# A four-layer graph network on one core: x3 transposed through HBM, softmax and RMS factors spread from compact bf16 parts

## The chip, the core and the metric

The kernel runs on one core of a Trainium2 chip. A core has a matrix engine (TensorE, PE in the profile), which multiplies a stationary operand held in its array (loaded by a weight load, PEld) with a moving operand, and writes to PSUM; VectorE (DVE); ScalarE (ACT); GpSimd (POOL); and SyncE (SP), which here issues every DMA. Each engine works through its own queue in order. The metric is the device time of one execution in microseconds, the median of several.

## What is computed

There are 32 graphs of 512 nodes with 256 features. `adj` holds zeros and ones, with ones on the diagonal. Every graph goes through four layers, and each ends in `x = layernorm(x + layer(x))`. All of it is float32.

```
L0: q,k,v = x@Wq+bq, x@Wk+bk, x@Wv+bv        # 8 heads of 32
    p = softmax(where(adj>0, q@k.T/sqrt(32), -9e15));  L0 = (p@v)@Wo + bo
L1: L1 = relu(((1+eps)*x + adj@x)@W1 + b1)@W2 + b2              # hidden 512
L2: h = (eps*x + adj@x)@W1 + b1                                 # hidden 1024
    L2 = silu(h * rsqrt(mean(h*h) + 1e-6) * rms_weight)@W2 + b2
L3: xn = layernorm(x)*gamma + beta;  A = s_out * adj * s_in
    L3 = softplus(xn@W_self + ((I - A)@xn)@W_neigh)
```

x3 is the input of layer 3. The two factors of this text are the reciprocal of the softmax sum, one per head and node, and the `rsqrt` of the mean square in L2 (the RMS factor), one per node.

## The kernel before

The 512 nodes are four tiles of 128 (`NT`), the 256 features two chunks of 128 (`DC`). The function `graph(b)` does not issue anything. It records operations, each with an engine (or two to choose from), a cost in nanoseconds, what it reads and writes, its buffers and a stage name. The class `Order` (L60) then puts the operations of all 32 graphs in one order with a list scheduler: among those that can start within 100 ns of the earliest on an engine, the one with the lowest key goes first. A key is the graph's number times `PERIOD`, plus a place between the earliest and the latest time at which the operation could stand within its graph (`LATE`), plus a number per stage (`LEAD`); `TURN` is the cost that the scheduler puts down when TensorE goes from whole-array products to row tiles (scores) or column tiles (p@v), `TURN_DUE` a penalty on such a turn, `HASTE` moves the last graph. So stages of several graphs lie interleaved on every engine, and the order that results is the program's order.

The parts that matter here, with their lines:

- **Scores and softmax** (`attend`, L751): for each half of the heads (`g`) and each node tile four products of 32 rows run side by side in the array (L766, tile `sc`). VectorE adds the mask and takes the row extremum (L790), ScalarE takes the exponential and its sum `rs` (L804). VectorE turns 32x32 blocks of the result (L840), SP writes them to an HBM scratch `via` (L852) and reads them back as `pT` (L864), and TensorE multiplies with v in 32-column tiles (L883, tile `po_att`).
- **Softmax factor** (stage `rinv`, L897 to L957), once for each `g`: VectorE takes the reciprocal of 16 sums per row (L903) and splits it into three bf16 parts whose sum keeps the float32 precision (L912, L919). The parts are written with gaps into a 128 x 4 x 128 tile `parts`, which TensorE transposes in four products (L930, `pm_t`); the result is copied (L937 or L938); one product with the 0/1 selector `sel_r` spreads it over the 32 rows of each head (L943, `pr_r`, 512 columns); it is copied to `oT` (L533), and VectorE multiplies `po_att` into it (L955). `oT` is what the product with Wo reads (L970, `po<-wo,oT`).
- **RMS factor** (stage `rms`, L1245 to L1298): TensorE sums squares (L1251, `pm`), VectorE and GpSimd make the factor `rr`, VectorE writes four diagonal matrices (L1275, `diag`), and one float32 product of a matrix of ones with them (L1281, `pb`) puts the factor of each node into every row. VectorE multiplies it into eight blocks of `gT` (L1289), ScalarE takes silu in two halves (L1304), then comes W2 (L970, `po<-w,gT`).
- **x3 transposed** (stage `x3T`, L1332 to L1360): eight float32 transposes on TensorE (L1341, `pt`), two copies out of PSUM by VectorE or ScalarE (L1352, L1356) into `xnT`, which the first product of layer 3 reads (L1369, `pz`). It is followed by the product with adj (L1411, `pa_l`).
- **Transposes by DMA that exist already**: for every graph but the first, `load_blocks` (L577) reads x and adj from HBM in 32x32 blocks whose runs are 128 bytes, four DMAs a matrix, and VectorE turns the blocks in place (L665 for x, L614 for adj).

```
def load_blocks(dst, src, q):
    v = src.rearrange("(i r) (m a c) -> a r m i c", r=32, a=4, c=32)
    nc.sync.dma_start(dst[32 * q : 32 * q + 32].rearrange("r m (i c) -> r m i c", c=32), v[q])
```

Of the kernel before, what the change touches and what calls it, by code (L numbers as in the profile page):

```python
# [9 lines left out]
F32 = mybir.dt.float32  # L10
BF16 = mybir.dt.bfloat16
AF = mybir.ActivationFunctionType
ALU = mybir.AluOpType
# [3 lines left out]
P = 128  # L17
# [2 lines left out]
RMS_EPS = 1e-6  # L20
HEADS = 8

PERIOD = 55957
LEAD = {
    "adjT": 178900, "agg1": 2600, "agg2": -164100, "degree": 73600, "diag": -115600,
    "lap": -139200, "ln0": -34000, "ln1": -303400, "ln2": 108900, "ln3": 310600, "load": 67000,
    "move": -461200, "pv": -4100, "pz": -65900, "qk": 9400, "rinv": -98900, "rms": -72400,
    "scores": -4600, "silu": 110900, "softplus": 52400, "v": 134300, "w11": 4200, "w12": -5600,
    "w21": -3500, "w22": -9100, "wo": -16600, "x3T": -71100, "xT": -89500,
}  # L30


# [27 lines left out]
class Order:  # L60
# [8 lines left out]
    WAIT = 70  # L69
    TABLE, TABLE_DUE = 1300, 9000  # L70

    TURN = {"whole": 93, "row": 200, "col": 93}
    TURN_DUE = 6000
    LATE = 0.85
    HASTE = 12445

    def __init__(self):
        self.ops = []
# [204 lines left out]
def kernel(  # L283
# [53 lines left out]

    ident_b = const.tile([P, P], BF16, name="ident_b")  # L340
    nc.vector.tensor_copy(ident_b, ident)
    parts = []
    for i in range(2):
        t = const.tile([P, NT, P], BF16, name=f"parts{i}")
        nc.gpsimd.memset(t, 0.0)
        parts.append(t)
    id_js = ident.rearrange("p (j s) -> p j s", s=HD)
    block = const.tile([P, HPG], F32, name="block")
    nc.vector.tensor_reduce(block, id_js, axis=AX.X, op=ALU.add)
    rows_js = const.tile([P, HPG], F32, name="rows_js")  # L350
    nc.vector.tensor_reduce(rows_js, id_js[:, :, 0:3], axis=AX.X, op=ALU.add)
    rows_of = const.tile([P, 1], F32, name="rows_of")
    nc.vector.tensor_reduce(rows_of, rows_js, axis=AX.X, op=ALU.add)
    sel_r = const.tile([P, HPG, HD], BF16, name="sel_r")
    nc.vector.tensor_scalar_mul(
        sel_r, block.unsqueeze(2).to_broadcast([P, HPG, HD]), rows_of[:, 0:1]
    )

    order = Order()

# [138 lines left out]
    def graph(b):  # L499
        first, last = b == 0, b == B - 1  # L500
        early = b < 1
        def op(ways, r=(), w=(), hold=()):
            order.op(b, ways, r, w, hold, stage[0])
# [3 lines left out]
        def bank(name):  # L507
            return Buf(ps, [P, 512], F32, "m", f"{name}_{b}", 4)

        def tmp(shape, tag, bufs, name=None, dtype=F32):  # L510
            return Buf(sb, shape, dtype, tag, f"{name or tag}_{b}", bufs)

        def pe(cost, fn, r, w, *hold, turn="whole"):

            op([("PE", cost, fn, {"turn": turn})], r, w, hold)

        def dve(cost, fn, r, w, port=False):
            op([("DVE", cost, fn, {"port": 1} if port else {})], r, w)
# [7 lines left out]
        def either(r, w, dve_way, act_way, port=False):  # L526
            op([("DVE", dve_way[0], dve_way[1], {"port": 1} if port else {}), ("ACT", act_way[0], act_way[1], {})], r, w)
# [32 lines left out]
        def small(name, bufs=2, shape=None):  # L560
            return Buf(sb, shape or [P, NT], F32, "s_" + name, f"{name}_{b}", bufs)
# [186 lines left out]

        oT = tmp([P, DC, N], "oT", 1)

        def attend(g):  # L751


            mx = small("mx", 2, [P, NT, HPG])
            rs = small("rsum", 2, [P, NT, HPG])
            po = bank("po_att")
            pTs = []
            for t in range(NT):
# [21 lines left out]
                for j in range(HPG):  # L780
# [5 lines left out]
                    else:  # L786
# [18 lines left out]
                            row(), row(), AF.Exp,  # L805
                            bias=mx[:, t, j : j + 1],
                            scale=-1.0,
                            accum_out=rs[:, t, j : j + 1],
                        ),
                        [(mx, t, j)], [(pq, j), (rs, t, j)],  # L810
                        table="exp",
                    )
                stage[0] = "move"
# [81 lines left out]
                )  # L895

            stage[0] = "rinv"  # L897

            tj = [(t, j) for t in range(NT) for j in range(HPG)]
            rv = small("rv", 2, [P, NT, HPG])  # L900
            dve(
                240,
                lambda: nc.vector.reciprocal(rv(), rs()),  # L903
                [(rs, t, j) for t, j in tj], [(rv,)],
            )
            part = parts[g].rearrange("p t (j s) -> p t j s", s=HD)
            left = rv
            for r in range(3):
                dst = part[:, :, :, r]
                dve(  # L910
                    190,
                    lambda dst=dst, left=left: nc.vector.tensor_copy(dst, left()),  # L912
                    [(left,)], [("parts", g), ("parts", g, r)], port=True,
                )
                if r < 2:
                    rest = small("rest", 2, [P, NT, HPG])
                    dve(
                        180,
                        lambda dst=dst, left=left, rest=rest: nc.vector.tensor_tensor(  # L919
                            rest(), left(), dst, ALU.subtract  # L920
                        ),
                        [(left,), ("parts", g, r)], [(rest,)], port=True,
                    )
                    left = rest
            pm_t = Buf(ps, [P, N], BF16, "m", f"pm_t_{b}", 4)
            mT = tmp([P, N], "mT", 2, dtype=BF16)

            def tr():
                for t in range(NT):
                    nc.tensor.transpose(  # L930
                        pm_t[:, t * P : (t + 1) * P], parts[g][:, t, :], ident_b
                    )

            pe(240, tr, [("parts", g)] + [("parts", g, r) for r in range(3)], [(pm_t,)], mT)
            either(
                [(pm_t,)], [(mT,)],
                (420, lambda: nc.vector.tensor_copy(mT(), pm_t())),  # L937
                (590, lambda: nc.scalar.copy(mT(), pm_t())),  # L938
            )
            pr_r = bank("pr_r")  # L940
            pe(
                130,
                lambda: nc.tensor.matmul(  # L943
                    pr_r(),
                    lhsT=sel_r.rearrange("p j e -> p (j e)"),
                    rhs=mT(),
                    start=True,
                    stop=True,
                ),
                [(mT,)], [(pr_r,)], oT,  # L950
            )
            evacuate(lambda: oT[:, g, :], pr_r, [(pr_r,)], [(oT, g)])
            dve(
                700,
                lambda: nc.vector.tensor_tensor(oT[:, g, :], po(), oT[:, g, :], ALU.mult),  # L955
                [(po,)], [(oT, g)],
            )  # L957

        def pair_sum(lhs, lhs_k, w, w_k, nk, y, step):

# [101 lines left out]
        values()  # L1062
        attend(0)
        attend(1)
        stage[0] = "wo"
        pair_sum(oT, lambda k: (oT, k), wo, "wo", DC, y, DC)

# [200 lines left out]
        rr = small("rr")  # L1268
        rsqrt(rr, ms, [(ms,)], [(rr,)])

        diag = tmp([P, NT, P], "sq", 2, "diag")

        def spread():
            for t in range(NT):
                nc.vector.tensor_scalar_mul(diag[:, t, :], ident, rr[:, t : t + 1])  # L1275

        dve(880, spread, [(rr,)], [(diag,)])
        pb = bank("pb")
        pe(
            870,  # L1280
            lambda: nc.tensor.matmul(  # L1281
                pb(), lhsT=ones, rhs=diag().rearrange("p t q -> p (t q)"), start=True, stop=True
            ),
            [(diag,)], [(pb,)],
        )
        for m in range(C2):
            dve(
                750,
# [41 lines left out]
        r3 = small("r3")  # L1330
        rsqrt(r3, v3e, [(v3e,)], [(r3,)])
        stage[0] = "x3T"  # L1332
        xnT = tmp([P, DC, N], "hT", 1, "xnT")
        for c in range(DC):
            pt = bank("pt")
            for rt in row_tiles:
                part = slice(rt[0] * P, (rt[-1] + 1) * P)

                def tr_x3(c=c, rt=rt, pt=pt):
                    for t in rt:  # L1340
                        nc.tensor.transpose(  # L1341
                            pt[:, t * P : (t + 1) * P], x3[:, t, c * P : (c + 1) * P], ident
                        )

                pe(115 * len(rt), tr_x3, [(x3, t) for t in rt], [(pt, rt[0])], xnT)
                src = lambda part=part, pt=pt: pt[:, part]
                dst = lambda part=part, c=c: xnT[:, c, part]
                op(
                    [
                        (  # L1350
                            "DVE", 160 + 133 * len(rt),
                            lambda src=src, dst=dst: nc.vector.tensor_copy(dst(), src()), {},  # L1352
                        ),
                        (
                            "ACT", 190 + 100 * len(rt),
                            lambda src=src, dst=dst: nc.scalar.copy(dst(), src()), {},  # L1356
                        ),
                    ],
                    [(pt, rt[0])], [(xnT, c, t) for t in rt],
                )  # L1360

        stage[0] = "pz"
        zy = tmp([P, NT, 2 * D], "aT", 1, "zy")
# [160 lines left out]
```

## Time and profile before

| what | value |
|---|---|
| median of three runs | 3435.14 us (3434.87 to 3435.78) |
| the profiled execution's own time | 3424.53 us |
| its span, first to last instruction | 3422.5 us |
| PE / DVE / ACT / POOL busy | 98% / 78% / 59% / 25% of the span |
| mean busy share of the 16 DMA engines by the one queue that carries the data | 66.9% |
| HBM read, written | 364.27 MB, 276.82 MB |

A row of a group of instructions reads: line, engine, operation, tiles written and read, shape, count, then busy time, mean duration of one, and the idle time of the engine just before them with what ended it. A matmul's own duration holds its way through the array, and the next one starts before it ends; so the time that one costs is read from the starts of two neighbours in the timeline, whose rows give start, duration, line, tiles and count. Each float32 product of the program stands in the profile as two passes.

### The profile page before, as it was taken

The page shows a single profiled execution, that of the slowest core. Times are in us where ns is not written, and L with a number is a line of the kernel's source. Part 1 is how long each engine was busy: PE and PEld are TensorE (multiplying, and loading weights), DVE is VectorE, ACT ScalarE, POOL GpSimd, SP SyncE. Part 2 cuts the span into 40 slices and gives each one's busy share as a digit, 9 for nine tenths or more (in the row PEclk, how much of TensorE's full clock was granted, in tenths as well). Part 3 has the DMA queues.
Part 4 walks back from the last instruction along what each step waited for, and adds up shares of the span by engine and source line. Part 5 has one row for each costly group of instructions (what it writes and reads, how often), then busy time and mean ns, then how long its engine had stood idle before and what let it go on. Part 6 is the DMA issues. An engine that isn't in the chain of part 4 may idle for free.

```text
span 3422.5 us, 55733 instructions
## 1 busy us (share of the span) xinstructions
PE 3368.0 (98%) x20000; PEld 2030.2 (59%) x20000; DVE 2664.6 (78%) x6241; ACT 2033.0 (59%) x4124; POOL 857.9 (25%) x615
## 2 busy tenths in 40 slices
PE   8999999999999999999999999999999999999997
PEld 5556655665655666556655655565566655565565
DVE  7788878778777788777787777887877877778755
ACT  6555666556666556666566655666565666556633
POOL 1222222222232222222132321222222223212231
PEclk9999999999999999999999999999999999999999
DMA  5777766667767667666677666676766767766710
GB/s 152 231 220 215 207 195 191 197 186 213 198 186 199 194 197 202 195 189 197 187 212 198 186 191 200 194 204 190 197 191 191 215 191 196 192 196 180 207 40 13
DMA packets 622868, 644.74 MB, mean 188 GB/s; under 512 B 410752, under 2 KB 446976, under 8 KB 590848
## 3 DMA queue, kind: packets, MB, share of 16 engines
q1 hardware_dynamic: 622592, 641.19, 66.9%
q8 instruction: 157, 2.57, 0.3%
q14 instruction: 119, 0.97, 0.1%
HBM read 364.27 MB, written 276.82 MB: 187 GB/s over the span
## 4 chain that ended last, share of the span: by engine, by line
PE 89%; DMA 5%; DVE 3%; issue 1%; SPq 1%; ACT 1%; POOL 0%; DVEq 0%; POOLq 0%
PE po L970 22%; PE ph L1148 13%; PE pg L1165 7%; PE sc L766 7%; PE pq L694 7%; PE pa L1165 7%; PE pz L1369 7%; PE pa_l L1411 6%; PE po_att L883 6%; DMA adjT<-in_adj_dram 4%; PE pv L735 3%; PE pb L1281 1%; PE pt L1341 1%; DVE pq L790 1%; PE pm L1251 1%
## 5 line engine op out<-in xcount | busy, mean ns | idle before, releaser
L804 ACT ACTIVATE pq<-pq,mx 128x512 f32<-128x512 f32 x1024 | 728.1, 712 | 255.9 <-DVE mx L790 161.0
L790 DVE CUSTOM_DVE_ANT_0 pq<-sc,bias 128x512 f32<-128x512 f32 x1024 | 664.0, 684 | 151.0 <-PE sc L766 95.3
L840 DVE STREAM_TRANSPOSE pq<-pq 128x2048 f32<-128x2048 f32 x248 | 572.2, 2307 | 82.7 <-ACT pq L804 82.5
L970 PE MATMUL po<-w,gT 128*128 128x256 f32 x2048 | 466.6, 381 | 0.5 <-ACT gT L1304 0.5
L1165 PE MATMUL pg<-hT,w 128*128 128x512 f32 x1024 | 465.9, 598 | 0.0
L970 PEld LDWEIGHTS po<-w,gT 128*128 128x128 f32 x2048 | 384.4, 190 | 88.8 <-issue 36.9
L540 POOL TENSOR_TENSOR ssq<-ssq,sq 128x512 f32<-128x512 f32 x220 | 281.1, 1278 | 292.1 <-ACT sq L1241 285.1
L1023 POOL TENSOR_TENSOR rstd<-ve,nhalf 128x4 f32<-128x4 f32 x132 | 143.7, 1089 | 767.9 <-DVE ve L1018 767.8
L1165 PEld LDWEIGHTS pg<-hT,w 128*128 128x128 f32 x1024 | 189.4, 190 | 218.6 <-issue 206.0
L766 PE MATMUL sc<-kT,qT 32*128 32x512 f32 x2048 | 292.1, 640 | 5.3 <-DVE nmr L1030 4.4
L883 PEld LDWEIGHTS po_att<-pT,v 128*32 128x32 f32 x8192 | 215.8, 110 | 94.9 <-issue 66.8
L883 PE MATMUL po_att<-pT,v 128*32 128x128 f32 x8192 | 250.2, 274 | 0.0
L1369 PE MATMUL pz<-wsn,xnT 128*128 128x512 f32 x512 | 236.7, 597 | 0.4 <-DVE xnT L1352 0.4
L540 POOL TENSOR_TENSOR sp<-sp,y 128x1024 f32<-128x1024 f32 x31 | 73.0, 2355 | 645.6 <-PE pg L1165 572.5
L1165 PE MATMUL pa<-hT,w 128*128 128x512 f32 x512 | 233.3, 599 | 0.3 <-DVE hT L532 0.3
L1148 PE MATMUL ph<-adjT,y_att 128*128 128x512 f32 x512 | 227.3, 596 | 1.4 <-DVE adjT L1130 1.4
L1148 PE MATMUL ph<-adjT,y 128*128 128x512 f32 x512 | 228.5, 598 | 0.0
L970 PE MATMUL po<-w,aT 128*128 128x256 f32 x1024 | 227.6, 379 | 0.0
L1411 PE MATMUL pa_l<-zy,adjT 128*128 128x256 f32 x1024 | 226.6, 379 | 0.0
L1411 PEld LDWEIGHTS pa_l<-zy,adjT 128*128 128x128 f32 x1024 | 194.5, 190 | 40.8 <-issue 15.5
L970 PEld LDWEIGHTS po<-w,aT 128*128 128x128 f32 x1024 | 192.0, 190 | 26.5 <-ACT pq L804 0.8
L804 ACT ACTIVATION_READ_ACCUMULATOR pq<-pq,mx 128x1 f32 x1024 | 191.9, 187 | 0.0
(150 smaller groups left out, 4991.6 us busy)
## 6 DMA issues: line engine op xcount, KB each, us to landing
via<-pq SPq DMA_DIRECT2D x992, 256.0 KB, 4.3
pT<-via SPq DMA_DIRECT2D x248, 1024.0 KB, 5.7
adj<-in_adj_dram SPq DMA_DIRECT2D x32, 1024.0 KB, 5.1
adjT<-in_adj_dram SPq DMA_DIRECT2D x124, 256.0 KB, 4.7
x<-in_x_dram SPq DMA_DIRECT2D x32, 512.0 KB, 3.9
xT<-in_x_dram SPq DMA_DIRECT2D x124, 128.0 KB, 4.1
out_dram<-sp SPq DMA_DIRECT2D x31, 512.0 KB, 5.2
w<-in_L_gnn_W_dram SPq DMA_DIRECT2D x2, 1024.0 KB, 6.5
```

The costliest lines, as they stand in the source:

```text
L540: lambda: nc.gpsimd.tensor_tensor(dst(), dst(), src(), ALU.add), {},
L694: nc.tensor.matmul(pq(), lhsT=w[:, c, m * P : (m + 1) * P], rhs=xT[:, c, :], start=(c == 0), stop=(c == DC - 1),)
L766: nc.tensor.matmul(sc[:, j, :], lhsT=qT[hp, g, t * P : (t + 1) * P], rhs=kT[hp, g, :], start=True, stop=True,)
L790: lambda t=t, j=j, sc=sc, row=row: nc.vector.tensor_tensor_reduce(out=row(), in0=sc[:, j, :].rearrange("p (a n) -> p a n", a=4), in1=bias[ ...
L804: lambda t=t, j=j, row=row: nc.scalar.activation(row(), row(), AF.Exp, bias=mx[:, t, j : j + 1], scale=-1.0, accum_out=rs[:, t, j : j + 1],),
L840: lambda pq=pq: nc.vector.transpose(pq().rearrange("p a j c s -> p (a j c s)"), pq().rearrange("p a j c s -> p (a j c s)"),),
L883: nc.tensor.matmul(po[j * HD : (j + 1) * HD, t * P : (t + 1) * P], lhsT=v[:, c, h * HD : (h + 1) * HD], rhs=pT[:, :, j, c, :], start=(c == 0),
L970: nc.tensor.matmul(po[:, i * D : (i + 1) * D], lhsT=lhs[:, k, t * P : (t + 1) * P], rhs=w[:, k, :], start=(i == 0 and k == 0), stop=(i == ...
L1148: nc.tensor.matmul(ph(), lhsT=xin[:, m, c * P : (c + 1) * P], rhs=adjT[:, m, :], start=(m == 0), stop=(m == NT - 1),)
L1165: nc.tensor.matmul(pa(), lhsT=w[:, c, m * P : (m + 1) * P], rhs=hT[:, c, :], start=(c == 0), stop=(c == DC - 1),)
L1369: nc.tensor.matmul(pz(), lhsT=xnT[:, c, t * P : (t + 1) * P], rhs=wsn[:, c, :], start=(c == 0), stop=(c == DC - 1),)
L1411: nc.tensor.matmul(pa[:, i * D : (i + 1) * D], lhsT=adjT[:, m, t * P : (t + 1) * P], rhs=zy[:, m, D : 2 * D], start=(m == 0), stop=(m == N ...
```

## The change

Three things are changed, and the scheduler's numbers with them.

1. x3, for every graph but the last, is written by one DMA to an HBM scratch tensor `x3d` and read back by four `load_blocks` DMAs; VectorE turns the blocks in place. Its tile `xnT` takes the buffer of `xT` instead of that of `hT`.
2. The softmax factor is made once per graph for both halves (32 sums per row). Its three bf16 parts lie side by side in 96 columns; one transpose gives 96 rows, and eight products of 128 columns, four per half, spread them with a wider selector. `po_att` itself is now copied to `oT` at once, and the product with the factor is taken from PSUM later.
3. The RMS factor goes the same way: three parts in 12 columns, one transpose, four products of 128 columns with a selector `sel_t`. The diagonal matrices and the float32 product of ones are gone.

`PERIOD`, all of `LEAD`, `TURN`, `TURN_DUE`, `LATE` and `HASTE` have other values, so the order of all engines is another one.

```diff
-PERIOD = 55957
+PERIOD = 65676
...
-    TURN = {"whole": 93, "row": 200, "col": 93}
-    TURN_DUE = 6000
-    LATE = 0.85
-    HASTE = 12445
+    TURN = {"whole": 93, "row": 290, "col": 150}
+    TURN_DUE = 500
+    LATE = 0.06
+    HASTE = -1245
...
+    NX = 2 * NT * HPG
+    sel_r = selector(NX, HD, "sel_r")
+    sel_t = selector(NT, P, "sel_t")
...
             stage[0] = "rinv"
+            evacuate(lambda: oT[:, g, :], po, [(po,)], [(oT, g)])
+
+        def split(src, n, name):
+            parts = tmp([P, 3, n], "p_" + name, 2, name + "p", dtype=BF16)
...
+            pe(
+                65,
+                lambda: nc.tensor.transpose(
+                    pm_t[0 : 3 * n, :], parts().rearrange("p r x -> p (r x)"), ident_b
+                ),
...
+            mT = split(rv, NX, "sums")
+            for g in range(2):
...
+                    for t in range(NT):
+                        x = (g * NT + t) * HPG
+                        nc.tensor.matmul(
+                            pr_r[:, t * P : (t + 1) * P],
+                            lhsT=sel_r[0 : 3 * NX, x : x + HPG].rearrange("p j e -> p (j e)"),
+                            rhs=mT[0 : 3 * NX],
+                            start=True,
+                            stop=True,
+                        )
...
-        dve(880, spread, [(rr,)], [(diag,)])
...
+        mT = split(rr, NT, "rms")
+            for t in range(NT):
+                nc.tensor.matmul(
+                    pb[:, t * P : (t + 1) * P],
+                    lhsT=sel_t[0 : 3 * NT, t],
+                    rhs=mT[0 : 3 * NT],
+                    start=True,
+                    stop=True,
+                )
...
+            x3d = Buf(dr, [N, D], F32, "x3d", f"x3d_{b}", 2)
+                    lambda: nc.sync.dma_start(
+                        x3d().rearrange("(t p) d -> p t d", p=P), x3()
+                    ),
...
+                        "SP", 4900, lambda q=q: load_blocks(xnT(), x3d(), q),
...
+                lambda: nc.vector.transpose(
+                    xnT().rearrange("p c i -> p (c i)"), xnT().rearrange("p c i -> p (c i)")
+                ),
```

## The prediction

> **What bounds the kernel now.** I read the page's busy shares first, then the three steady windows of about one graph each, then TensorE's timeline.
>
> ```profile
> PE 3368.0 (98%) x20000; PEld 2030.2 (59%) x20000; DVE 2664.6 (78%) x6241; ACT 2033.0 (59%) x4124; POOL 857.9 (25%) x615
> ...
> 1500.00:1607.00 107.00, 106.01 (x631) 63.44 (x624) 83.80 (x196) 65.33 (x131) 27.01 (x19) 1.00 0.71 195
> 1607.00:1714.00 107.00, 106.84 (x627) 63.85 (x626) 84.88 (x200) 66.14 (x132) 28.70 (x20) 1.00 0.69 195
> 1714.00:1821.00 107.00, 105.66 (x625) 63.34 (x624) 83.94 (x197) 64.98 (x134) 27.67 (x20) 1.00 0.71 198
> ```
>
> The columns of the windows after their length are PE, PEld, DVE, ACT, POOL, then TensorE's granted clock and DMA share. A busy PE alone proves little, since a pass's duration overlaps the next one's. But here PE stands still only 0.2 to 1.3 us of 107, at full clock, with DVE 22 us idle. The timeline shows the passes packed:
>
> ```profile
> 1528.93 1.12 PE L1281 MATMUL pb<-diag,ones 128*128 128x512 f32 x2
> 1529.89 2.31 PE L1148 MATMUL ph<-adjT,y_att 128*128 128x512 f32 x5
> ...
> 1545.74 0.39 PE L930 MATMUL pm_t<-ident_b,parts 128*128 128x128 bf16 x4
> 1545.96 1.95 PE L970 MATMUL po<-w,gT 128*128 128x256 f32 x8
> 1547.74 0.38 PE L943 MATMUL pr_r<-mT,sel_r 128*128 128x512 bf16 x1
> 1547.96 1.89 PE L970 MATMUL po<-w,gT 128*128 128x256 f32 x8
> 1549.78 1.14 PE L766 MATMUL sc<-kT,qT 32*128 32x512 f32 x8
> 1550.85 5.45 PE L970 MATMUL po<-w,gT 128*128 128x256 f32 x24
> ...
> 1569.14 1.04 PE L1341 MATMUL pt<-ident,y 128*128 128x128 f32 x8
> 1570.01 7.07 PE L970 MATMUL po<-w,aT 128*128 128x256 f32 x32
> 1576.92 1.88 PE L694 MATMUL pq<-xT,wq 128*128 128x512 f32 x4
> ```
>
> Start to start, 32 passes of `po` take 1576.92 - 1570.01 = 6.91 us (0.216 each), each with its own weight load, which hides. So TensorE's issue time is the time of the kernel, and a nanosecond taken from it counts until another engine is late. The same reading prices a change of array mode: the eight `po` passes before `sc` take 1549.78 - 1547.96 = 1.82 us. At 0.216 each, eight are 1.73. The turn costs 0.09 us.
>
> **Part 1, what TensorE loses.** From start to start:
> - x3's eight transposes: 1570.01 - 1569.14 = 0.87 us, 31 graphs: 27.0 us.
> - `pb`, two passes in float32: 1529.89 - 1528.93 = 0.96 us, 32 graphs: 30.7 us.
> - `pm_t`, four bf16 transposes: 0.22 us, 64 times: 14.1 us.
> - `pr_r`, one pass of 512 columns: 0.22 us, 64 times: 14.1 us.
>
> Together 85.9 us.
>
> **Part 2, what TensorE gets.** Two transposes, eight softmax products and four RMS products per graph, all bf16 with 128 columns. Nearest row: `pm_t`, four load and product pairs of just this size in 0.22 us, 0.055 each. 14 x 0.055 x 32 = 24.6 us. The Trainium skill, TensorE: Matmul & The Clock Gate, section Back-to-back issue gap, speaks against this: it gives about 81 ns per product of 128 columns in a stream of load and product pairs. By it, 14 x 0.081 x 32 = 36.3 us, 12 us more. The row is of this kernel, so I take 0.055 and keep 36 for the range.
>
> The four RMS products have 12 rows, and the built program gives them a 32-row tile, as for the scores. The scheduler counts them as whole-array work, so it pays no attention to the turn. They stand amid `pa_l`, so one turn in and one out: 2 x 0.09 x 32 = 5.8 us. Their pace in that mode no row shows. Lower end 0.055. Upper end 0.14: `sc` takes 1.07 us for two rounds of 512 columns with the turn out, some 0.08 above two whole-array passes of 0.43 and that turn, which I read as a second weight load that no longer hides. bf16 weights load in 98 ns against 182 (groups of `parts` and `sc`), so I take 0.095: 4 x 0.04 x 32 = 5.1 us on top.
>
> The order of the program turns the array 829 times after, 678 before. 64 of the 151 are those just priced; 87 x 0.09 = 7.8 us more.
>
> Sum on TensorE: -85.9 + 24.6 + 5.8 + 5.1 + 7.8 = -42.6 us.
>
> **Part 3, what lies beside it.** VectorE loses 128 diagonals (30.1 us), 31 copies of `xnT` (21.4) and half the reciprocals; it gains 31 turns of `xnT`, each like that of `xT` (1243 ns): 38.5 us, and 63 small copies. The casts and rests keep their number, 192 and 128. More comes from the new order, which moves work from ACT: 58 copies of `oT`, 31 each of `diag` and `adjT`, 53 normalised `y` and others. Counted with the durations of before, DVE goes from 2665 to about 2755 us, ACT falls by about 190. DVE then has some 20 us idle per graph, so this costs nothing unless it comes in a bad place.
>
> On SP, every graph adds one write and four reads. What is queued behind them:
> - `x3d` waits for x3 normalised; behind it stand a `via` write and `pT` read. The reads of x3d stand seven entries later in SP's order, two to three score tiles on. The eight tiles of a graph share 105 us (the chain's `ph` rows at 643.40, 747.66 and 852.43), 13 us each, against a landing of some 4 us for 512 KB (`x`, 3.9). SP doesn't stand still for the landing.
> - The turn of `xnT` on DVE waits for the reads, one score tile after the `via` write issued just before them. Behind it in DVE's queue are the four mask-and-extremum operations of the next score tile, then `zy<-pz`. The nearest row:
>
> ```profile
> adjT<-in_adj_dram SPq DMA_DIRECT2D x124, 256.0 KB, 4.7
> x<-in_x_dram SPq DMA_DIRECT2D x32, 512.0 KB, 3.9
> xT<-in_x_dram SPq DMA_DIRECT2D x124, 128.0 KB, 4.1
> ```
>
> 128 KB in 128-byte runs land 4.1 us after issue. The way from that `via` write is its issue (2 us for four), one `pT` issue, four issues and 4.1: about 8 us, of 13. About 4 us is left before DVE stops. The Trainium skill, DMA: Bandwidth & Descriptors, Rules for kernel authors, advises against exactly this: a transpose by a plain DMA with a rearranged pattern is put 19 times behind the hardware's. By it 3.9 us for 512 KB would become 74 us, far past the cover, some 60 us of stall per graph. But the change doesn't rearrange elements, VectorE does; the `xT` row is the same function on the same shape, and its wait costs DVE 8.5 us in all (its group). I take nothing; the bounds are nothing and the rival below. The DMA engines get 1 MB more per graph, 32.5 on 641 MB (+5%), but 127k more packets on 623k (+20%): their share goes from 67% to between 70 and 80%.
>
> **Part 4, stalls that are there.** The largest wait of PE is `po<-wo,oT` for VectorE's last product into `oT`:
>
> ```profile
> L970 PE MATMUL po<-wo,oT 128*128 128x256 f32 x512 | 122.3, 385 | 17.0 <-DVE oT L955 16.9
> L1341 PE MATMUL pt<-ident,y 128*128 128x128 f32 x256 | 34.7, 278 | 4.2 <-DVE y L1041 4.0 <-DVE v3e L1326 0.2
> ```
>
> After, the factors are ready before the second half's p@v; behind its last pass come the copy of `po_att` (0.69), a cast (0.19) and the product (0.69), with latencies about 1.9 us, while TensorE has `pz` and one score tile (1.72 + 1.16). That is 1 us of cover; the stall may shrink. The silu chain, from `pb` to the first `po<-w,gT`: four products of 0.67 (L1289) and 1.9 us of silu, with 0.6 to start, some 5.3 us, against `pa_l` 5.2, `sc` 1.1 and `po<-wo` 0.9 after: 7.1. Also covered, by less than before, where `ph` and p@v stood between. Both margins are 1 to 2 us, so I count the stalls as unchanged, with 15 us either way. In the last graph the cover is `pa_l` alone, 3.5 us against 5.3 (6.9 before): +2 us.
>
> **Sum.** 3424.5 - 42.6 + 2 = 3384 us against the profiled execution. The median stands 10.6 us above that execution, so 3394 us, -1.2%.
>
> **The rivals.** What a measurement of this kernel can tell from no change is about 0.2%, 7 us (3428 to 3442).
> - *Bigger gain* (0.15). The 17 us of `oT` stalls and other small ones go as well, since softmax factors are early: 3394 - 25 = 3369. For it: the cover counted above. Against: DVE is fuller.
> - *Little is left* (0.20). Short passes run at the page's 81 ns (+12) and the chains with 1 us of margin each lose 0.3 to 0.7 us a graph (10 to 22 us): 3416 to 3428. A little more gives no change. For it: two chains and thinner cover before `po<-w,gT`.
> - *Slower* (0.08). The turn of `xnT` waits for x3d. Place: DVE's queue, ahead of the next tile's four extrema. From about 4 us of lateness DVE stands, then ACT, then TensorE for lack of scores and `pz`. It decides once TensorE loses more than 1.4 us per graph (42/31). If the reads of x3d land in the longest time that one of `adjT` took, 10.5 us, 6.4 above the 4.1 counted, less 4 of cover, 2.4 us a graph are lost: 3394 + 31 x 2.4 = 3468. Against it: DVE is kept only 55 us in all by the block reads of adj.
> - *The change doesn't do what it says*: the transposes stay. The order shows 8 in all after, 256 before, so no.
>
> **How the numbers follow.** Likeliest, 0.57: 3394, between 3378 and 3412. With bigger gain and little left, 3364 to 3430 holds about 8 in 10 and more; beyond are slower and part of no change. Faster by over 0.2%: 0.86; within: 0.07; slower: 0.07 (the rival's milder forms fall within).
>
> **What would show it.** Right: `pt` gone but for 8 passes, `pr_r` and `pm_t` at 0.055 us start to start, graphs 103.5 us apart instead of 105, PE at 98% still. The RMS products between two turns of 0.09. Wrong: idle of PE or of DVE ended by `xnT<-x3d`; `po<-w,gT` waiting for silu; a pace of the short passes above 0.1 us; DVE near 90%.

## The result, and the profile after

After: 3420.06 us (median of 6, 3413.53 to 3427.03). Before, in the same comparison: 3435.01 us (6 runs, 3427.07 to 3437.59). The ratio is 0.9961, 95% interval [0.9945, 0.9976]: 15 us faster, where 41 had been forecast. The profiled execution took 3417.82 us, with a span of 3416.0 (before 3424.53 and 3422.5), so between the two profiles there are only 6.7 us to explain (6.5 by the spans).

The busy shares and two steady windows of the kernel after (columns as before: PE, PEld, DVE, ACT, POOL, clock, DMA share; the last is GB/s):

```profile
PE 3336.3 (98%) x19816; PEld 1997.2 (58%) x19816; DVE 2734.7 (80%) x6373; ACT 1852.4 (54%) x3804; POOL 861.6 (25%) x610
```

```profile
1500.00:1604.50 104.50, 103.39 (x615) 61.65 (x614) 85.09 (x198) 57.56 (x119) 27.35 (x20) 1.00 0.80 207
1604.50:1709.00 104.50, 104.01 (x620) 61.80 (x622) 85.13 (x199) 57.83 (x119) 27.69 (x21) 1.00 0.79 209
```

VectorE, ScalarE and the DMA share went where the forecast put them (DVE 2735 for about 2755, ACT down by 181, DMA 0.75 over the run), and the page still says 98% for PE. But the groups, with the idle time before them behind the second bar, show a wait that was not there before. Two rows of the kernel before, then four of the kernel after:

```profile
L1369 PE MATMUL pz<-wsn,xnT 128*128 128x512 f32 x512 | 236.7, 597 | 0.4 <-DVE xnT L1352 0.4
L614 DVE STREAM_TRANSPOSE adjT<-adjT 128x1024 f32<-128x1024 f32 x62 | 73.9, 1226 | 55.0 <-DMA adjT<-in_adj_dram 55.0
```

```profile
L1410 PE MATMUL pz<-wsn,xnT 128*128 128x512 f32 x512 | 243.6, 616 | 32.0 <-DVE xnT L1395 31.9
L981 PE MATMUL po<-wo,oT 128*128 128x256 f32 x512 | 135.9, 391 | 0.0
L1395 DVE STREAM_TRANSPOSE xnT<-xnT 128x1024 f32<-128x1024 f32 x31 | 38.6, 1245 | 58.8 <-DMA xnT<-x3d 58.7
L613 DVE STREAM_TRANSPOSE adjT<-adjT 128x1024 f32<-128x1024 f32 x62 | 73.6, 1224 | 90.8 <-DMA adjT<-in_adj_dram 90.8
```

Read the third row of the kernel after and then the first: the reads of x3d are late (58.7 us of VectorE), so the turn of `xnT` is late, so `pz` is (32 us of TensorE). In the second row the 17 us for `oT` are gone. VectorE's wait for adjT was 55.0 us before and is 90.8 now. The DMA rows, whose last number is the median time from issue to landing, say the same:

```profile
adjT<-in_adj_dram SPq DMA_DIRECT2D x124, 256.0 KB, 6.6
x<-in_x_dram SPq DMA_DIRECT2D x32, 512.0 KB, 6.3
xT<-in_x_dram SPq DMA_DIRECT2D x124, 128.0 KB, 7.7
x3d<-y SPq DMA_DIRECT2D x31, 512.0 KB, 8.4
xnT<-x3d SPq DMA_DIRECT2D x124, 128.0 KB, 6.7
```

The 128 KB block reads, which I had at 4.1 us from the row of xT, take 6.7 and 7.7. The timeline of the short passes on TensorE in the kernel after:

```profile
1619.73 1.13 PE L981 MATMUL po<-wo,oT 128*128 128x256 f32 x4
1620.79 0.22 PE L924 MATMUL pm_t<-ident_b,rmsp 128*12 128x128 bf16 x1
1620.94 1.99 PE L1452 MATMUL pa_l<-zy,adjT 128*128 128x256 f32 x8
1622.87 0.39 PE L1288 MATMUL pb<-mT_rms,sel_t 12*128 12x128 bf16 x4
1623.19 5.45 PE L1452 MATMUL pa_l<-zy,adjT 128*128 128x256 f32 x24
```

`pb`'s four passes take 1623.19 - 1622.87 = 0.32 us: four at 0.056 and the turn out of the 32-row mode, 0.09. The turn into it is in the row above: eight passes in 1.93 us, where 8 x 0.216 = 1.73. Half of the 0.20 more is the turn (the last of the eight takes 0.31), half stands behind `pm_t` (the first takes 0.32). The row of `pm_t` shows what the prediction did not name: the transpose of 12 columns also stands between two turns. From it to `pa_l` are 0.15 us instead of 0.056, and the four passes ahead of it take 1.06, 0.09 more than in e9_best below, where that turn is taken out. The prediction's count of turns held them all the same: going by the tile shapes in the trace, TensorE changes 829 times between whole-array passes and tiles of at most 32 rows or columns, and 704 times in e9_best.

All of TensorE, as the sum of times from one start to the next, in us (a wait falls to the pass ahead of it; the last column is an experiment below, in which no transfer is late):

| passes | before | after | both reorderings |
|---|---|---|---|
| `pt`, `pb`, `pm_t`, `pr_r` | 91.3 | 39.8 | 39.6 |
| `pa_l` (holds turns for the RMS products) | 221.1 | 235.1 | 235.1 |
| `pg` and `pz` (hold the wait for `xnT`) | 680.7 | 722.3 | 678.4 |
| `po` (holds the waits for `oT`) | 810.2 | 800.7 | 799.6 |
| span | 3422.5 | 3416.0 | 3363.6 |

In the first two rows, which hold the passes that were changed, TensorE's time fell by 51.5 - 14.0 = 37.5 us, near the forecast 42.6. Of the 14.0, the passes next to the RMS transpose and products take about 9, 28 turns into scores 2.6, and one wait for silu in the last graph 1.7. The third row of the table gives the 37.5 back.

### The profile page after: what moved, and what is told of

It is laid out like the page before. It is cut to its first block, busy times and chain, and to the rows that moved or that the text cites. A ratio compares the mean times of both kernels' runs of the same rounds, so it can differ in the third digit from the quotient of the medians.

```text
span 3416.0 us, 55265 instructions
## 1 busy us (share of the span) xinstructions
PE 3336.3 (98%) x19816; PEld 1997.2 (58%) x19816; DVE 2734.7 (80%) x6373; ACT 1852.4 (54%) x3804; POOL 861.6 (25%) x610
## 2 busy tenths in 40 slices
DMA packets 768194, 677.23 MB, mean 198 GB/s; under 512 B 540208, under 2 KB 592304, under 8 KB 736176
## 4 chain that ended last, share of the span: by engine, by line
PE 79%; SPq 8%; DMA 6%; DVE 5%; ACT 1%; issue 1%; POOL 0%; DVEq 0%; POOLq 0%; ACTq 0%
PE po L981 16%; PE ph L1160 13%; SPq L579 8%; PE pz L1410 7%; PE pa L1177 7%; PE sc L766 6%; PE pq L693 6%; PE po_att L883 6%; PE pg L1177 6%; PE pa_l L1452 6%; PE pv L734 3%; DMA xnT<-x3d 3%; DMA adjT<-in_adj_dram 2%; DVE xnT L1395 1%; DVE adjT L613 1%; DVE st L1021 1%
## 5 line engine op out<-in xcount | busy, mean ns | idle before, releaser
L1034 POOL TENSOR_TENSOR rstd<-ve,nhalf 128x4 f32<-128x4 f32 (+1 forms) x132 | 132.2, 1001 | 609.4 <-DVE ve L1029 608.7
L1410 PE MATMUL pz<-wsn,xnT 128*128 128x512 f32 x512 | 243.6, 616 | 32.0 <-DVE xnT L1395 31.9
L1452 PE MATMUL pa_l<-zy,adjT 128*128 128x256 f32 x1024 | 238.3, 386 | 0.0
L1253 ACT ACTIVATE sq<-gT 128x512 f32<-128x512 f32 x224 | 140.2, 626 | 128.0 <-DVE gT L1232 120.6
```

The costliest lines, as they stand in the source:

```text
L1410: nc.tensor.matmul(pz(), lhsT=xnT[:, c, t * P : (t + 1) * P], rhs=wsn[:, c, :], start=(c == 0), stop=(c == DC - 1),)
L1452: nc.tensor.matmul(pa[:, i * D : (i + 1) * D], lhsT=adjT[:, m, t * P : (t + 1) * P], rhs=zy[:, m, D : 2 * D], start=(m == 0), stop=(m == N ...
```

## The experiments

**Where a graph's reads of x3d lose their time.** SP's queue of one graph after; times in us, issue is how long SP was held by it:

| start | issue | transfer | landed |
|---|---|---|---|
| 1800.12 to 1801.61 | 0.30 to 1.19 | `via`, four writes, 256 KB each | 1807.23 |
| 1802.97 | 1.00 | `pT`, one read, 1 MB | 1811.74 |
| 1805.41 | 0.58 | `xnT<-x3d`, first of four reads | 1812.39 |
| 1806.03 | 0.67 | second | 1813.31 |
| 1806.75 | 4.17 | third | 1814.09 |
| 1810.96 | 0.86 | fourth | 1814.93 |

From the first write to the last landing: 2.85 to the `pT` read, 2.44 to the first read of x3d (it waits 1.4 us for the last q and k product to leave `xT`'s buffer), 5.55 to the start of the fourth, 3.97 to its landing. That is 14.8 us, where I had 8. Two suspects: the shared buffer, and the third issue, which is held for 4.2 us. Theory A says that the late reads are the loss. The rivals were a fuller TensorE (turns), and DMA engines that are simply full.

**e1_own**: a buffer of its own for `xnT`. **e2_early**: the same, and the four reads three entries earlier in SP's queue. To make room, both leave out the bias rows of layers 0 and 2 and one diagonal constant (others stand in for them), so their output is not that of the layers above; e4_both and e8_most below do the same.

```diff
-        xnT = tmp([P, DC, N], "hT" if last else "xT", 1, "xnT")
+        xnT = tmp([P, DC, N], "hT" if last else "xn", 1, "xnT")
...
+            before = ahead[-places]
+            out = [o for o in out if o not in reads]
+            i = out.index(before)
+            out[i:i] = reads
```

> The changed kernel with a buffer of its own for xnT and every engine's order kept, so that the block reads of x3d no longer wait until q and k have been made from xT. To make room, the bias rows of layers 0 and 2 are left out (layer 1's row stands in for them) and one diagonal constant serves for both. Theory A, TensorE waits some 1.2 us a graph (36 us in all) because the reads go out late: if the buffer is what holds them (1.4 us from wait to issue), the turn of xnT comes over 1 us earlier and the time falls by about 30 us, to 3390. If the queue is what holds them (the third of the four issues lasts 4.2 us, behind the 1 MB read of pT), the last block lands when it did and the time falls by 0 to 8 us, 3412 to 3420. Rival B, another chain is just as late as xnT and takes over its wait: 3420.

> As the run before it (own buffer, the same two things left out), and the four block reads stand three entries earlier in SP's queue: ahead of the via write and the pT read that they stood behind, right after the read of adj. Nothing else moves. Theory A: the blocks land some 10 us before the turn, DVE and TensorE no longer wait for them, the 36 us go: about 3385, with pz starting 0.43 us after the last pg. Rival B (a second chain as late): 3415 to 3420, with the idle time now at another product. Rival C (it is the load on the DMA engines as such, 75% busy, that makes everything late): the reads now delay the via write and pT, and the time stays at 3420 or rises.

Measured: e1_own 3445.99 us (ratio 1.0038 [1.0025, 1.0051]), e2_early 3393.27 (0.9894 [0.9875, 0.9913]). The shared buffer is not the cause. In e1_own the reads go out right behind the `pT` read and the third is still held, 4.8 us in the graph I looked at. Its TensorE waits more than the changed kernel's: from `pg` to `pz` 57.1 us against 50.1, from p@v to `ph` 28.6 against 13.4. Why adjT is later there (112.5 us of VectorE against 90.8) I did not settle. In e2_early the blocks land 11.5 us ahead of the turn, and the wait for `xnT` is gone from TensorE. What remains is listed by its waits (total, times, longest):

```profile
PE ph L1184 <- ACT y_att L1084: 22.2, 21, 3.1
PE ph L1184 <- ACT y L1084: 4.9, 2, 2.7
```

So 45 us of TensorE's waits went against the changed kernel (36.4 from `pg` to `pz`, 8.8 between passes of `pz`), and 13 more stand at `ph<-y_att` (from p@v to `ph` 26.4 us against 13.4). They did not come with the early reads: e1_own has 28.6 there already, and e6_x3 below, which keeps the shared buffer, 14.9.

**e3_whole**: the RMS factor's transpose and spread use all 128 columns and rows, padded with zeros, so the array isn't turned. **e4_both**: this and e2_early.

```diff
-                    pm_t[0 : 3 * n, :], parts().rearrange("p r x -> p (r x)"), ident_b
+                    pm_t[0:rows_n, :],
+                    wide[b % 2] if name == "rms" else parts().rearrange("p r x -> p (r x)"),
+                    ident_b,
...
-                    lhsT=sel_t[0 : 3 * NT, t],
-                    rhs=mT[0 : 3 * NT],
+                    lhsT=sel_t[:, t],
+                    rhs=mT(),
```

> The changed kernel with the RMS factor's transpose and spread done over all 128 columns and rows (zeros in the rest), so that TensorE doesn't turn to a narrower tile for them; same order. The trace of the changed kernel shows 0.09 us extra before and after the 12-column transpose and before and after the 12-row products. Theory D, these four turns are real work on TensorE's path: 4 x 0.09 x 32 = 11.5 us less, 3408. Rival: the wait for xnT sets the pace and swallows what is saved elsewhere: 3418 to 3420.

> Own buffer, early block reads and whole-array RMS factor together (layer 1's bias row in place of those of layers 0 and 2, as before). If A and D hold and add up: 3385 - 11 = 3374. If another chain is late behind xnT: near 3400 or above.

Measured: 3416.04 us (0.9952 [0.9939, 0.9964]) and 3398.76 (0.9906 [0.9892, 0.9921]). Both misses: the turns left TensorE (`pa_l` and `pb` are shorter), the time did not follow. Here `ph<-y_att` took it: from p@v to `ph` 25.1 us in e3_whole (13.4 in the changed kernel), 39.9 in e4_both (26.4 in e2_early). What is that second wait? The timeline of e3_whole ahead of one such `ph`:

```profile
1414.23 7.68 SPq L585 DMA_DIRECT2D adjT<-in_adj_dram  x3
...
1426.67 2.37 DVE L619 STREAM_TRANSPOSE adjT<-adjT 128x1024 f32<-128x1024 f32 x2 [5.26 <-DMA adjT<-in_adj_dram]
...
1428.96 0.65 DVE L1007 TENSOR_TENSOR y_att<-po,y_att 128x512 f32<-128x512 f32 x1
...
1432.31 1.02 POOL L1046 TENSOR_TENSOR rstd<-ve,nhalf 128x4 f32<-128x4 f32 x1 [9.30 <-DVE ve L1041]
...
1433.42 0.13 DVE L1053 SCALAR_TENSOR_TENSOR nmr<-mv,rstd 128x4 f32<-128x4 f32 x1
...
1433.59 1.09 ACT L1072 ACTIVATE y_att<-y_att,nmr,rstd 128x256 f32<-128x256 f32 x2 [2.33 <-DVE nmr L1053]
...
1434.24 3.27 PE L1172 MATMUL ph<-adjT,y_att 128*128 128x512 f32 x7 [2.07 <-ACT y_att L1072]
```

VectorE stands 5.26 us for adjT's blocks. Behind the turn in its queue stands the layer norm of `y_att`, and `ph` waits for that norm. The name on TensorE's wait is ScalarE's; the timeline puts the cause with a DMA, the same mechanism at a second place, and e5_adj below tries it. And adjT's reads are held too: in SP's queue four reads of xT and a `pT` read stand ahead of them.

**Three reorderings of SP's queue**, nothing else moved. **e5_adj**: where xT's four reads, a `pT` read and adjT's four reads follow each other, adjT's go first and xT's last (28 graphs), so adjT's come ahead of the `pT` read too. **e6_x3**: x3d's reads ahead of the `pT` read. **e7_two**: both. **e8_most**: e2_early with adjT's reads moved as in e5_adj.

```diff
+            if [out[i].stage for i in at] == ["xT"] * 4 + ["move"] + ["adjT"] * 4:
+                new = [out[i] for i in at[5:] + at[4:5] + at[:4]]
...
+            before = sp[sp.index(reads[0]) - 1]
+            if before.stage != "move":
+                continue
+            out = [o for o in out if o not in reads]
+            i = out.index(before)
+            out[i:i] = reads
```

> The changed kernel, one change in the order of the DMA queue: the four block reads of adjT and the four of xT that stand in front of them trade places, 28 graphs; every other engine's order is that of the changed kernel. Theory A (a block read that lands late keeps VectorE standing before its turn, and what stands behind the turn in VectorE's queue, here the layer norm of y_att, is late for TensorE): adjT lands some 4 us earlier since 512 KB of xT no longer stand in front, VectorE's wait for adjT falls from 91 us to below 40, ph's wait for y_att (13 us of TensorE) to below 4: about 3410 us. Rival B (the sixteen DMA engines are simply full, and order only chooses which transfer is late): xT or pT waits in its place, 3416 to 3424. Rival C (the norm of y_att is late by the work on VectorE and ScalarE themselves): the wait for adjT falls, the one for y_att stays, 3416 to 3422.

> The changed kernel, one change in the order of the DMA queue: the four block reads of x3d stand ahead of the pT read (1 MB) that stood right before them, 30 graphs; xnT still takes xT's buffer, nothing is left out. Theory A: the reads no longer wait for the issue of the third one (4.2 us in the changed kernel) and land about 3.5 us earlier; pz's wait for xnT falls from some 36 us to below 15, of which about 8 come back at ph<-y_att: about 3398 us. Rival B (the engines are full, pT is late in its place and po_att waits): 3415 to 3425. Rival D (the reads are late because they wait for the last q and k product to free xT's buffer, not because of the queue): the landing moves by less than 1 us, 3414 to 3422, or slower where pT is now kept behind that wait.

> Both reorderings of the DMA queue in one kernel, nothing left out. Theory A: the two gains add, since they are two waits at two places: about 3385 us, TensorE standing for xnT and y_att below 15 us together. Rivals: B 3412 to 3424; if only the one of x3d works, 3398; if only that of adjT, 3410.

> The kernel with a buffer of its own for xnT and its reads three entries earlier, with the bias rows of two layers left out and stood in for by another's, as before, and now adjT's block reads ahead of xT's. It was at 3393 us without that, with TensorE waiting 26 us for y_att at ph. Theory A: VectorE's wait for adjT falls from 111 us to below 50, ph's wait for y_att to below 8: about 3376 us. Rival C (the norm is late by the work of VectorE and ScalarE): ph's wait stays at 20 us and more, 3388 to 3396. Rival B: 3390 to 3400 with another transfer late.

Measured: e5_adj 3404.96 us (0.9927 [0.9911, 0.9943]), e6_x3 3374.62 (0.9841 [0.9821, 0.9862]), e7_two 3366.53 (0.9815 [0.9797, 0.9833]), e8_most 3367.05 (0.9815 [0.9796, 0.9834]). Theory A's predictions hold, and each gain is larger than I expected. In e5_adj from p@v to `ph` are 5.5 us instead of 13.4. VectorE's wait for adjT, in the changed kernel and in e5_adj (total, times, longest):

```profile
DVE adjT L613 <- DMA adjT<-in_adj_dram: 90.8, 29, 4.4
DVE adjT L624 <- DMA adjT<-in_adj_dram: 20.0, 25, 1.9
```

In e6_x3 the four issues of a graph take 2.05 us to the start of the last, 5.71 in the changed kernel (medians per graph); the first read still goes out 24.8 us after x3d has landed, as in the changed kernel. Its DMA row and its group of `pz`:

```profile
xnT<-x3d SPq DMA_DIRECT2D x124, 128.0 KB, 3.6
```

```profile
L1425 PE MATMUL pz<-wsn,xnT 128*128 128x512 f32 x512 | 235.6, 602 | 0.4 <-DVE xnT L1379 0.3
```

The blocks land 1.7 us before the turn instead of being waited for, with the shared buffer kept and with the same 1 MB a graph more. So neither the buffer nor full DMA engines was the cause. In e7_two the chain that ended last is TensorE's again, and two windows show it busy all through, at 103.00 us:

```profile
PE 95%; DVE 2%; DMA 2%; ACT 1%; SPq 0%; issue 0%; POOL 0%; POOLq 0%; DVEq 0%; ACTq 0%
```

```profile
1500.00:1603.00 103.00, 103.00 (x617) 61.99 (x616) 86.29 (x199) 57.77 (x119) 27.32 (x19) 1.00 0.80 210
1603.00:1706.00 103.00, 103.00 (x617) 61.99 (x616) 86.03 (x199) 57.89 (x119) 27.32 (x19) 1.00 0.77 210
```

In the changed kernel that chain was PE 79%, SPq 8%, DMA 6%, DVE 5%. e8_most, with its own buffer, is no better than e7_two without.

**e9_best**: e7_two with e3_whole's padding.

> Both reorderings of the DMA queue (366.5 us over 3000 before this edit: 3366.5) and the RMS factor's transpose and spread over all 128 columns and rows, with zeros, so that TensorE's array is not turned for them. Nothing left out. In the changed kernel the same edit was worth 4 us only, and nothing in the kernel with the early reads. Theory A (the turns cost TensorE 0.38 us a graph, 12 us in all, and so far the waits for y_att behind adjT's late blocks took the gain): those waits are gone, so about 3355. Rival (what the turns cost on TensorE is not what sets the time): 3363 to 3370.

Measured: 3352.88 us (0.9777 [0.9764, 0.9791]), 14 us below e7_two. With no late transfer to take it, the gain of the turns shows. It is faster than both kernels of this study and leaves nothing of the computation out. Its timeline beside that of the changed kernel above:

```profile
1585.47 1.13 PE L1019 MATMUL po<-wo,oT 128*128 128x256 f32 x4
1586.44 0.22 PE L960 MATMUL pm_t<-ident_b,wide 128*128 128x128 bf16 x1
1586.49 1.95 PE L1490 MATMUL pa_l<-zy,adjT 128*128 128x256 f32 x8
1588.28 0.39 PE L1326 MATMUL pb<-mT_rms,sel_t 128*128 128x128 bf16 x4
1588.50 5.40 PE L1490 MATMUL pa_l<-zy,adjT 128*128 128x256 f32 x24
```

From `pm_t` to the last `pa_l` of this stretch: 1588.50 - 1586.44 = 2.06 us, against 1623.19 - 1620.79 = 2.40; with 0.09 saved ahead of it 0.43 us, and with 0.05 in the first pass behind it (0.27 instead of 0.32) 0.48 us a graph.

**The x3 part undone.** Does this part pay for itself as it stands? **e10_pe** puts the eight transposes back on TensorE and lets the scheduler plan again:

```diff
-        xnT = tmp([P, DC, N], "hT" if last else "xT", 1, "xnT")
-        if last:
+        xnT = tmp([P, DC, N], "hT", 1, "xnT")
+        if True:
```

> The changed kernel with its x3 part undone: x3 is transposed by TensorE in every graph again and xnT takes the buffer of hT, as before; the compact factors stay; the scheduler places the transposes (just ahead of one score tile and pz). Theory A (in the changed kernel the late reads of x3d cost about what the transposes on TensorE cost, or more): TensorE gets 27 us back, the waits for xnT (36 us at pg to pz, about 9 between the pz passes) go, adjT's blocks land earlier by less traffic: 3398 to 3412, not slower than the changed kernel. Rival (the x3 part is a clear gain as it stands, and the loss against the forecast lies in the factors): 3435 to 3447.

Measured: 3823.02 us (1.1147 [1.112, 1.1173]). It tells nothing about the x3 part: the new plan has other orders on every engine, with waits of 50 to 72 us for `y_att` and `gT` at TensorE and a mean granted clock of 0.952, where the changed kernel has 0.996. A second try holds every engine's order by hand, **e11_held**, and **e12_held_adj** with adjT's reads first:

```diff
-                        "SP", 4900, lambda q=q: load_blocks(xnT(), x3d(), q),
+                        "SP", 4900, lambda q=q: q or (behind.append(turned_by_pe)),
...
+                pt = ps.tile([P, HPG, N], F32, tag="s", name=f"pt_{b}", bufs=1)
+                for c in range(DC):
+                    for t in range(NT):
+                        nc.tensor.transpose(
+                            pt[:, c, t * P : (t + 1) * P], x3[:, t, c * P : (c + 1) * P], ident
+                        )
+                    nc.vector.tensor_copy(xnT[:, c], pt[:, c])
```

> The changed kernel with its x3 part undone by hand, and the order of every engine held this time: no write and no reads of x3d, no turn on VectorE; TensorE's eight transposes stand two product pairs ahead of the score tile before pz and use the banks of a score tile, VectorE copies them to xnT twice. The compact factors stay. Theory A (as it stands, the x3 part costs in late reads what it saves in transposes): 3420 + 27 for the transposes - 36 and 9 for the waits for xnT = 3402; with the wait for y_att behind adjT as before or up to 10 more, 3402 to 3412. So undoing this part makes the changed kernel no slower. Rival (the x3 part is a clear gain as it stands, and the loss against the forecast lies in the factors): 3435 to 3447.

> The same, and adjT's block reads ahead of xT's in the DMA queue. Beside the kernel with both reorderings (3366.5) it differs in the x3 part alone, with no transfer late in either. Theory A: the x3 part is worth its forecast 27 us once its reads are in time, so 3393, 3388 to 3400 with small waits for the banks. Rival (something else on TensorE or VectorE holds both): 3366 to 3375.

Measured: 3437.61 us (1.0024 [1.0017, 1.0031]) and 3427.08 (0.9993 [0.9985, 1.0001]), 30 us above what I expected. The waits showed a flaw of my own:

```profile
PE pt L1406 <- DVE xnT L1409: 24.3, 31, 0.8
```

The fifth transpose waits for the first copy, since both use one tile of PSUM. **e13_held** and **e14_held_adj** have both copies behind the eighth transpose:

```diff
                         )
+                for c in range(DC):
                     nc.vector.tensor_copy(xnT[:, c], pt[:, c])
```

> The changed kernel with its x3 part undone and every engine's order held, as in the try before, but both copies to xnT behind the eighth transpose. That try stood at 3437.6 us, of which some 38 were the experiment's own (65 us from transposes on, 27 without a wait). Theory A (as it stands the x3 part costs in late reads what it saves): 3437.6 - 38 = about 3400, 3395 to 3410, so the changed kernel without this part is faster than with it. Rival (it pays as it stands, the forecast fell short elsewhere): above 3420.

> The same with adjT's block reads ahead of xT's. The try before stood at 3427.1. Theory A (in time, the x3 part is worth its forecast 27 us): 3366.5 + 27 = 3393, 3386 to 3400. Rival (something else limits both): below 3378; or the transposes cost more than the row says: above 3405.

Measured: 3410.18 us (0.9938 [0.9925, 0.9951]) and 3397.87 (0.9905 [0.9891, 0.9918]). So the changed kernel is 8 to 10 us faster without its x3 part than with it (3410 against 3420, or 0.9938 against 0.9961; measured in two comparisons, with runs from 3404.77 to 3413.36 and from 3413.53 to 3427.03, whose intervals against before overlap by a little), and in no case worse off. With the reads in time the same part is worth 3397.87 - 3366.53 = 31 us, a little more than the 27 forecast: from start to start the transposes put back take 35 us in e14_held_adj, where the kernel before had 27. e13_held is also the compact factors alone, under the new order: 23 us below before. Its DMA rows settle the rival of full DMA engines:

```profile
DMA packets 622868, 644.75 MB, mean 189 GB/s; under 512 B 410752, under 2 KB 446976, under 8 KB 590848
```

```profile
adjT<-in_adj_dram SPq DMA_DIRECT2D x124, 256.0 KB, 6.8
xT<-in_x_dram SPq DMA_DIRECT2D x124, 128.0 KB, 7.7
```

These are the packets of the kernel before, to one, and the blocks land in 6.8 and 7.7 us as in the kernel after. The longer landings come with the new order of the queue, not with the added traffic.

## Why the prediction was wrong, step by step

- **The failed step** is Part 3, the reads of x3d: "The way from that `via` write is its issue (2 us for four), one `pT` issue, four issues and 4.1: about 8 us, of 13", and then "I take nothing". The way measured 14.8 us. Its landing (3.97) was right. (The 74 us set against it take a factor over the hardware's transpose and put it on a plain read; the block reads landed in 3.6 us where nothing held them, in e6_x3.) Wrong was the price of issuing: four issues were counted at their own length (some 2.6 us), and behind a 1 MB read they took 6.4 with the third held for 4.2, which is over half of the 6.8 us too many. The wait for `xT`'s buffer (1.4 us), which I had not seen either, costs nothing by itself (e6_x3 keeps it). On TensorE the step cost 36.4 us from `pg` to `pz` and 8.1 between the passes of `pz` (both against e7_two): 44.5.
- The "slower" rival named this wait with its place and put the point of decision at 1.4 us per graph. The wait came at 44.5/31 = 1.44 us per graph, and still the kernel was faster, because another term helped (the next point). This was the first of the signs named for being wrong, VectorE idle until `xnT<-x3d`.
- **Stalls "unchanged, with 15 us either way"**. The 17 us for `oT` went, as the "bigger gain" rival had it. The wait for `y_att` behind adjT's late blocks came (from p@v to `ph` 13.4 us, 5.5 where nothing is late). I had compared adjT's wait with the new one ("kept only 55 us in all") without asking what the new order puts ahead of adjT's reads.
- The measured 3420 lies in the range of "little is left" (3416 to 3428), but by luck: its reasons did not come. The short passes ran at 0.056 us, not 0.081, and of its two chains `oT` has no wait left, the one through silu a wait of 2.9 us near the start and one of 1.6 in the last graph, where the forecast had 2.
- **TensorE's sum, -42.6**: measured -37.5 in the two rows of the table. The pace of 0.055 us for a short pass held, 0.056 measured for `pr_r` and for `pb` alike: the price of 81 ns that I kept as the upper end is not what these passes show, and the 5.1 us for a slower pace in the 32-row mode was not due. (Its upper end had a slip besides: the row of `sc` gives 1.07 - 0.86 - 0.09 = 0.12 us for the second weight load, not 0.08.) The turns cost somewhat more than priced. Of the 87 that the prediction put down at 7.8 us without a name, 61 are those of the 12-column transpose and 26 come with the new order (e9_best has 704 turns, the kernel before 678). The 125 turns that padding takes away would be 11 us at 0.09 each; it was worth 14, since the pass behind a turn is longer too.
- **VectorE's 90 us more "costs nothing unless it comes in a bad place"**: held; it has 17 us idle per graph in e7_two, with PE busy all through.
- **DMA**: 127k more packets forecast, 145k measured (768194 against 622868); the share, 75%, lies in the forecast range.
- **Sum**, in the profiled executions: forecast -40.5, measured -6.7. Against the 34 us between stand the 44.5 for `xnT`, some 8 for `y_att` and 5 for TensorE's sum, less the 17 for `oT`: 41. Some 7 us the other way lie in rows of passes that I did not take apart. Of the median's 15 us, 8 more lie in where each profile stands to its own median (before 10.6 below, after 2.2 below).

With both waits taken away the kernel stands at 3366.5, below the forecast 3394: 64 us under before, of which the profile has 58.8, the work of TensorE 37.5, the waits for `oT` and their like in `po` 10.6, and the rest small pieces of other rows.

## What to carry to other kernels

A transfer's cover is counted from the queue, not from the transfer: list what stands ahead of it, add the time for which each issue is held, and look for a large transfer right in front of small urgent ones. A turn or copy that waits for a DMA stops everything behind it on its engine, so the wait appears under another engine's name elsewhere; follow it back through that engine's queue. And when an edit that clearly saves work moves nothing (e3_whole, e4_both), look for the wait that grew by as much before calling the work free: with that wait gone it was worth its price (e9_best). To undo one part of a change, hold the order of everything else; e10_pe did not, and measured a plan.

## What the runs showed of the hardware

- **An issue can be held by an earlier large transfer.** In the changed kernel 91 issues of SP after the first 100 us lasted more than 2.5 us, 400 us in all; in the kernel before 11, 36 us; in e7_two 37, 130 us. 88 of the 91 are the second or third transfer behind a 1 MB `pT` read, and at the median such an issue ends 0.4 us (second) or 0.7 us (third) before that read lands. What holds them until then, the runs do not show. In e2_early, where a 1 MB read of adj stands ahead of x3d's four, the third is held as well (4.8 us at the median), with 11.5 us to spare. Four reads behind four `via` writes of 256 KB went out unheld (e6_x3).
- **A transpose of few columns turns the array.** 12 columns of a 128-row operand cost 0.09 us on the way in and out, as a product with 12 rows does, and 0.05 in the pass behind. A transpose of 96 columns costs nothing on the way in (the `ph` pass ahead of it takes its usual 0.43; behind it come scores, so its way out can't be told apart), and products of 96 rows nothing on the way out (0.056 to the next `pg`). Padding both to 128 with zeros takes the turns away.
- **The dearest block read was xT's, at 7.7 us, with 30 us of slack** in the graph I looked at, while adjT's, due at once, stood behind it. Letting adjT's reads go ahead of xT's and of the `pT` read between them was worth 15 us by the medians (3404.96 against 3420.06), 12 by the ratios to the kernel before (0.9927 and 0.9961); which of the two transfers mattered more was not tried.
